# Attention's row maxima as b + relu(a - b) on half the columns, with the relu on ScalarE, and the output bias as a row added by a matmul

## The chip, the core and the metric

The kernel runs on one core of one Trainium2 chip. The metric is the device time of one execution in microseconds (us), the median of several runs. The core's engines are named as in the profile: PE (matrix multiplication), DVE (VectorE, element-wise operations and reductions), ACT (ScalarE, functions of one input), POOL (GpSimd) and SP (here the queue that issues most DMAs). PEld is the loading of weights into PE.

## What is computed

The reference is one decoder layer on x of 8 x 512 x 512 in f32, with three parts, each followed by a layer norm of the sum:

```python
x = layernorm(x + mamba(x))                       # a state-space scan, 1024 channels, 16 states
x = layernorm(x + attention(x, ctx_1024, mask))   # 16 heads of 32
x = layernorm(x + experts(x))                     # 32 experts, 4 per token, and a shared one
```

The change touches the attention:

```python
scores = einsum('bnlh,bnph->bnlp', qm, km) / sqrt(32)
scores = where(mask, scores, -1e8)
attn = softmax(scores, axis=-1)
out = einsum('bnlp,bnph->bnlh', attn, vm)
out = out.reshape(B, L, 512) @ Wo.T + bo
```

The softmax needs the largest score of every row, over 512 keys, for each of 8 batches, 16 heads and 512 queries.

## The kernel before

`program` runs three stages: `layers` (the scan and the attention, up to about 3750 us), `experts`, and `finish`. Only `layers` is changed.

**The order of the work.** The main loop of `layers` goes over 16 chunks (8 batches, two halves of 256 positions each), and in each over 32 steps of the scan. A step has on DVE a multiplication `steps_in` (L494), the scan itself (L501) and a multiplication `collect` (L510), each over 1024 or 1028 columns; on ACT four exponentials, `decays` (L480), into one of two buffers `l_da`; and on PE matmuls (L521) that add up the states in `py`. Between these the loop puts side work: the attention of the batch before, as a list of `units`, each with a weight. A step takes as many units as its share of the weights allows. A unit runs its matmuls at once and gives back a function, its second half, which is issued when the next unit comes (`settle`); a second half may give back a third. The last batch has no scan beside it, and its units run one after the other. On top of this the framework orders the instructions of each engine by its own planner, so that neighbours in the source need not be neighbours in a queue. Every queue is worked off in order.

**The attention of a batch.** `sources` makes values and keys from the context; `keys` (L732) adds the bias and applies the mask on DVE (L741) and writes the keys to DRAM (`kd`, 512 x 512). `spread` (L799) brings the queries and keys of two heads into `qa` and `ka`, three buffers of each in turn. Head j takes 64 partitions: 32 with the head, one with the mask's fill (`filld`), and more for the maximum that is to be subtracted. For each of 8 pairs of heads and 4 blocks of 128 queries, `maximum` (L811) makes the scores of 128 queries and 512 keys for two heads with two matmuls (L819) into a PSUM tile of 128 x 1024, and its second half reduces them to two maxima on DVE (L821). `negate` brings the four blocks' maxima into a row of `qa`. Then `weigh` (L839) makes the same scores transposed (L845), ACT takes their exponentials into `eT` (L849), and `gather` (L853) multiplies with the values (L861). The maxima run six units ahead of the exponentials. The PSUM pool for scores, `l_pss`, has two buffers, which `maximum` and `weigh` share; `eT` has two buffers in pool `l_p2`; many tiles of 128 x 512 share two buffers under the name `row` in `l_p3`.

`output` (L908) multiplies with Wo (`dense`, L753, four matmuls at L756), adds x (L919) and then the bias (L920), which `l_bo` holds in all 128 partitions. `biases` (L1037 on) adds the values' bias, multiplied with Wo, to it (L1055). `prepare` (L432) multiplies with `w_dt`, 32 partitions of 1024 columns (L437).

Of the kernel before, what the change touches and what calls it, by code (L numbers as in the profile page):

```python
# [17 lines left out]
P = 128  # L18
# [14 lines left out]
NB = 4  # L33
NPB = 3

NH = 16
# [53 lines left out]
def layers(ctx, tc, a, x1d, filld, based, xbuf, arm):  # L90
# [88 lines left out]
    w_x = const("w_x", [P, CC, RANK + 2 * NST], rows(a["x_proj_w"]))  # L179
    w_dt = const("w_dt", [RANK, DI], a["dt_proj_w"])  # L180
    b_dt = const("b_dt", [P, CC], a["dt_proj_b"])
# [4 lines left out]
    bv = cp.tile([P, DC], F32, name="l_bv")  # L186
    bo = cp.tile([P, D], F32, name="l_bo")
    wg = cp.tile([P, DC, E], F32, name="l_wg")
# [47 lines left out]
    for i in range(NPB):  # L236
        qas.append(cp.tile([P, S], F32, name=f"l_qa{i}"))
        kas.append(cp.tile([P, S], F32, name=f"l_ka{i}"))
        for t in (qas[i], kas[i]):
            for r0 in (HD, 2 * HD + HD):  # L240
                nc.gpsimd.memset(t[r0 : r0 + HD], 1.0 if t is qas[i] else 0.0)
# [21 lines left out]
    def later_constants():  # L263

        nc.sync.dma_start(
            aneg.rearrange("p c j g -> p (c j) g"),
            a["A_log"].rearrange("(b c) (s g) -> (c s) b g", c=QP, s=NQ),
        )
        for i in range(NPB):
            for r0 in (HD + 1, 2 * HD + HD + 1):  # L270
                nc.sync.dma_start(
                    kas[i][r0 : r0 + 1, :].rearrange("p (c t) -> p c t", c=DC),
                    ones[0:1, :].unsqueeze(1).to_broadcast([1, DC, P]),
                )
        nc.sync.dma_start(bq, a["bq"])
        nc.sync.dma_start(bk, a["bk"])
        nc.sync.dma_start(bv, a["bv"].rearrange("(c p) -> p c", p=P))
        nc.sync.dma_start(bo, a["bo"].partition_broadcast(P))
        nc.sync.dma_start(wg, rows(a["wg"]))
# [152 lines left out]
    def prepare(q, f):  # L432

        ps = psm.tile([P, 2, T], F32, tag="mm", name="ps_dt")
        for i in range(2):
            c = 2 * q + i
            nc.tensor.matmul(  # L437
                ps[:, i, :], w_dt[:, c * P : (c + 1) * P], f["xd"][0:RANK, :], start=True, stop=True
            )
# [267 lines left out]
    def sources(b):  # L707
# [3 lines left out]
        def begin():  # L711
            load("Wv")
            st["cT"] = cT = quad("s2", "cT")
            nc.sync.dma_start(cT, rows(a["ctx"][b]))
            st["mk"] = mk = p1.tile([P, S], U8, tag="mk", name="mk")
            nc.sync.dma_start(mk, a["mask"][b : b + 1, :].to_broadcast([P, S]))
            kept[b] = [dp.tile([S, D], F32, tag="vd", name="vd"), dp.tile([D, S], F32, tag="kd", name="kd")]

# [13 lines left out]
        def keys(oc):  # L732
            if oc == 0 and b:
                load("Wq")
            w, cT = loaded["Wk"], st["cT"]
            ps = dense(lambda dc: w[:, dc, oc * P : (oc + 1) * P], lambda dc: cT[:, dc, :])

            def put():

                k = p3.tile([P, D], F32, tag="row", name="k")  # L740
                nc.vector.scalar_tensor_tensor(k, ps, bk[:, oc : oc + 1], st["mk"], ALU.add, ALU.mult)  # L741
                nc.sync.dma_start(kept[b][1][oc * P : (oc + 1) * P, :], k)

            return put
# [7 lines left out]

    def dense(lhs, rhs):  # L753
        ps = psm.tile([P, S], F32, tag="mm", name="ps_p")
        for dc in range(DC):
            nc.tensor.matmul(ps, lhs(dc), rhs(dc), start=(dc == 0), stop=(dc == DC - 1))  # L756
        return ps

    def units(b):
# [39 lines left out]
        def spread(i):  # L799
# [3 lines left out]
            for j in range(2):  # L803
# [4 lines left out]
                nc.sync.dma_start(ka[r1 + HD : r1 + HD + 1, :], filld[b : b + 1, :])  # L808
                nc.sync.dma_start(qa[r1 + HD + 1 : r1 + HD + 2, :], ka[r1 + HD + 2 : r1 + HD + 3, :])

        def maximum(i, lt):  # L811
# [5 lines left out]
            for j in range(2):  # L817
                r = slice(j * 2 * HD, (j + 1) * 2 * HD)
                nc.tensor.matmul(ps[:, j, :], qa[r, lt * P : (lt + 1) * P], ka[r, :], start=True, stop=True)  # L819
            mx = st["mx", i]  # L820
            return lambda: nc.vector.tensor_reduce(mx[:, lt, :].unsqueeze(2), ps, AX.X, ALU.max) and None  # L821

# [85 lines left out]
        def output(lt):  # L908
# [6 lines left out]
            w, attT = loaded["Wo"], st["attT"]  # L915
            pp = dense(lambda dc: attT[:, dc, lt * P : (lt + 1) * P], lambda dc: w[:, dc, :])

            def add_up():
                nc.vector.tensor_tensor(xr, pp, xr, ALU.add)  # L919
                nc.vector.tensor_tensor(st["x2"][lt], xr, bo, ALU.add)  # L920
                if lt == SC - 1:
                    return layernorm(nc, sm, st["x2"], st["x2"], "ln3")
# [114 lines left out]
    def biases():  # L1037
# [6 lines left out]
        nc.vector.tensor_scalar(fl[0:B, :], fl[0:B, :], -1.0, 1e8, ALU.add, ALU.mult)  # L1044
        nc.sync.dma_start(filld, fl[0:B, :])

# [3 lines left out]
        for dc in range(DC):  # L1050
# [3 lines left out]
            )  # L1054
        nc.vector.tensor_tensor(bo, bo, psb, ALU.add)  # L1055

# [538 lines left out]
def program(tc, a, out):  # L1595
    nc = tc.nc
    with tc.tile_pool(name="dram", bufs=1, space=DRAM) as dram, tc.tile_pool(name="one", bufs=1) as one:
        x1d = dram.tile([N, D], F32, name="x1d")
        filld = dram.tile([B, S], F32, name="filld")

# [42 lines left out]
```

## Time and profile before

| | us |
|---|---|
| runs (median, lowest, highest) | 5266.59, 5265.96, 5273.14 |
| profiled execution, its own time | 5280.81 |
| its span | 5279.1 |
| DVE busy in the span | 4173.3 |
| PE busy in the span | 4501.0 |
| ACT busy in the span | 2586.6 |
| L821, the maxima, 256 instructions | 309.8 |
| L849, the exponentials, 256 instructions | 258.7 |

The profile is of one execution. A group of instructions is given by its line in the kernel, its engine, its operation, the tile that it writes and those that it reads, the shapes and the count; then follow its busy time, the mean duration of one in ns, the engine's idle time before them, and what ended that idle time ("<-PE py L521" says that line 521 on PE did). A waits view adds up, for each pair of a waiting line and the line waited for, the time in total, the number of times and the longest. A timeline has the start, the length, the engine, the line and the operation, with the idle time before it in brackets. An f32 matmul appears as two records.

### The profile page before, as it was taken

Reading aid. Unit: us, or ns where it says so; the run is one execution under the profiler, and the core shown is the slowest. Engines: PE = TensorE matmul, PEld = TensorE weight load, DVE = VectorE, ACT = ScalarE, POOL = GpSimd, SP = SyncE. Lnnn points to the kernel's source line nnn. Section 1 sums busy time; section 2 is a strip of 40 time slices with the busy share of each in tenths; the row PEclk is TensorE's granted clock in tenths of the full one; section 3 lists DMA queues with packets and bytes.
Section 4 is the critical chain, followed back from the end, with each engine's and each line's share of the span. In section 5 each row is a group of like instructions: output and inputs, shape, how many; then the busy total and the mean of one; then the engine's idle time right before and its main releaser. Section 6 shows DMA issues by size and latency. Waiting matters only on the chain. (4 is left out here: it accounts for less than half of the span.)

```text
span 5279.1 us, 54371 instructions
## 1 busy us (share of the span) xinstructions
PE 4501.0 (85%) x17184; PEld 2464.4 (47%) x17184; DVE 4173.3 (79%) x5351; ACT 2586.6 (49%) x5771; POOL 588.5 (11%) x426
## 2 busy tenths in 40 slices
PE   6768889888888888888897888888899999999995
PEld 3324234333433433343342343332478888877774
DVE  7999898989989898998999899874355666656555
ACT  5565565665656556565655556533122333323233
POOL 1000002002000200200020020010112121111111
PEclk8879899999999999999999999999899999999997
DMA  8885345435533634544463554432244444444444
GB/s 236 266 229 157 72 119 177 115 101 148 160 95 91 208 88 109 171 128 102 105 201 78 125 173 113 106 115 93 93 129 125 128 139 132 128 116 132 117 123 151
DMA packets 486438, 711.64 MB, mean 135 GB/s; under 512 B 121576, under 2 KB 205064, under 8 KB 483952
## 3 DMA queue, kind: packets, MB, share of 16 engines
q1 hardware_dynamic: 449984, 626.90, 41.0%
q0 software_dynamic: 33280, 67.81, 5.8%
q10 hardware_dynamic: 2736, 11.54, 0.5%
q8 instruction: 221, 3.62, 0.3%
q14 instruction: 217, 1.78, 0.1%
HBM read 391.24 MB, written 164.79 MB: 105 GB/s over the span
## 5 line engine op out<-in xcount | busy, mean ns | idle before, releaser
L480 ACT ACTIVATE l_da<-rep,l_aneg 128x256 f32<-128x256 f32 x2048 | 893.5, 499 | 950.0 <-DVE h L501 885.6
L501 DVE TENSOR_TENSOR_SCAN h<-l_da,h 128x1028 f32<-128x1028 f32 x512 | 1163.3, 2285 | 21.6 <-ACT l_da L480 19.1
L494 DVE TENSOR_TENSOR h<-rep,bc 128x1024 f32<-128x1024 f32 x512 | 612.3, 1212 | 109.1 <-PE py L521 91.2
L510 DVE TENSOR_TENSOR h<-h,bc 128x1024 f32<-128x1024 f32 x512 | 616.8, 1211 | 2.1
L521 PE MATMUL py<-h,l_fold 128*32 128x512 f32 x2048 | 371.9, 649 | 108.1 <-DVE h L510 89.7
L819 PE MATMUL ps_s<-l_ka,l_qa 64*128 64x512 f32 x1024 | 331.8, 719 | 134.5 <-DVE mx L821 134.2
L1334 PE MATMUL ps_h<-xT,w 128*128 128x224 f32 (+3 forms) x1536 | 380.0, 397 | 38.4 <-issue 31.4
L1427 POOL DMA_INDIRECT based<-y,xe x160 | 272.5, 1703 | 1168.5 <-ACT y L1406 439.1
L821 DVE TENSOR_REDUCE mx<-ps_s 128x2 f32<-128x1024 f32 x256 | 309.8, 1214 | 67.8 <-PE ps_s L819 67.4
L861 PE MATMUL po<-eT,l_va 128*64 128x512 f32 x1024 | 302.5, 672 | 49.0 <-ACT eT L849 44.2
L1334 PEld LDWEIGHTS ps_h<-xT,w 128*128 128x128 f32 x1536 | 295.4, 193 | 103.8 <-issue 46.7
L845 PE MATMUL ps_t<-l_qa,l_ka 64*128 64x512 f32 x1024 | 305.5, 668 | 23.5 <-ACT eT L849 23.2
L849 ACT ACTIVATE eT<-ps_t 128x1024 f32<-128x1024 f32 x256 | 258.7, 1014 | 127.9 <-PE ps_t L845 127.8
L694 POOL DMA_INDIRECT xbuf<-x2t,dest x128 | 217.1, 1696 | 864.6 <-DVE dest L679 763.9
L343 PE MATMUL ps_z<-xnT,wm 128*128 128x256 f32 x1024 | 237.9, 389 | 28.4 <-DVE o L561 24.2
L756 PE MATMUL ps_p<-x2T,wa 128*128 128x512 f32 x512 | 241.9, 627 | 21.8 <-ACT hT L950 15.5
L552 PE MATMUL po<-wm,zs 128*128 128x512 f32 x512 | 248.5, 640 | 13.1 <-DVE z L963 11.8
L1334 PE MATMUL ps_h<-t,s 128*128 128x224 f32 (+3 forms) x1024 | 248.1, 393 | 5.8 <-DVE hT L1355 5.8
L1355 DVE TENSOR_TENSOR hT<-ps_h,p 128x224 f32<-128x224 f32 (+3 forms) x128 | 55.2, 432 | 248.9 <-PE ps_h L1334 248.8
L343 PE MATMUL ps_x<-xnT,wm 128*128 128x256 f32 x1024 | 245.7, 392 | 5.0 <-ACT xnT L332 3.2
L343 PEld LDWEIGHTS ps_z<-xnT,wm 128*128 128x128 f32 x1024 | 195.2, 193 | 90.2 <-DVE o L561 37.4
L343 PEld LDWEIGHTS ps_x<-xnT,wm 128*128 128x128 f32 x1024 | 195.8, 195 | 80.2 <-issue 43.7
(239 smaller groups left out, 6989.4 us busy)
## 6 DMA issues: line engine op xcount, KB each, us to landing
w<-in_w SPq DMA_DIRECT2D x93, 1024.0 KB
wm<-in_in_proj_w SPq DMA_DIRECT2D x128, 512.0 KB
rep<-dt SPq DMA_DIRECT2D x256, 256.0 KB
rep<-dtx SPq DMA_DIRECT2D x256, 256.0 KB
xbuf<-zero SPq DMA_DIRECT2D x32, 1362.5 KB
xe<-xbuf SPq DMA_DIRECT2D x32, 1362.5 KB
wm<-in_out_proj_w SPq DMA_DIRECT2D x64, 512.0 KB
wa<-in_sw SPq DMA_DIRECT2D x24, 1024.0 KB
```

The costliest lines, as they stand in the source:

```text
L343: nc.tensor.matmul(ps[:, i, :], w[:, dc, i * P : (i + 1) * P], f["xnT"][:, dc, :], start=(dc == 0), stop=(dc == DC - 1),)
L480: nc.scalar.activation(da[:, n, 1:], dt[:, j, i, :], AF.Exp, scale=aneg[:, 2 * q + i, 2 * jj + j, g : g + 1])
L494: nc.vector.tensor_tensor(h[:, :, 1:], dtx.rearrange("p j i t -> p (j i) t"), f["bc", g][0], ALU.mult)
L501: nc.vector.tensor_tensor_scan(flat, da.rearrange("p n t -> p (n t)"), flat, 0.0, ALU.mult, ALU.add)
L510: nc.vector.tensor_tensor(h[:, :, 0:T], h[:, :, 1:], f["bc", g][1], ALU.mult)
L521: nc.tensor.matmul(f["py"][j * QP : (j + 1) * QP, :, :], fold, hs[j // 2][:, 2 * (j % 2) : 2 * (j % 2) + 2, 0:T], start=False, stop=g == N ...
L819: nc.tensor.matmul(ps[:, j, :], qa[r, lt * P : (lt + 1) * P], ka[r, :], start=True, stop=True)
L821: return lambda: nc.vector.tensor_reduce(mx[:, lt, :].unsqueeze(2), ps, AX.X, ALU.max) and None
L845: nc.tensor.matmul(ps[:, j, :], ka[r, kc * P : (kc + 1) * P], qa[r, :], start=True, stop=True)
L861: nc.tensor.matmul(po[j * 2 * HD : (j + 1) * 2 * HD, :], va[:, kc, i, j * HD : (j + 2) * HD], eT[:, j, :], start=(kc == 0), stop=(kc == SC ...
L1334: nc.tensor.matmul(ps, w[:, n, r * P : (r + 1) * P], x[:, n, 0:cols], start=not more and n == 0, stop=n == 1, skip_group_check=more,)
L1427: put = nc.gpsimd.indirect_dma_start(out=based, out_offset=bass.IndirectOffsetOnAxis(ap=xe.bitcast(I32)[:, j, D + E :], axis=0), in_=ys[j] ...
```

## The change

The largest of two numbers is written as max(a, b) = b + relu(a - b). For each head, a is the scores of keys 0 to 255 and b those of keys 256 to 511. The keys in DRAM and in `ka`, and the mask's fill, get a third part of 256 columns that holds the first half less the second. The two matmuls of `maximum` then use columns 256 to 767 of `ka`, so that PSUM holds b and a - b. The second half of the unit takes relu(a - b) of both heads on ACT into `up`, a tile under the name `eT`; a new third part adds b and takes the maximum along the row on DVE, with one instruction per head.

The bias is no longer held in 128 partitions. It lies in one row, beside 31 rows of zeros, in a part of the tile of `w_dt`, which is made 64 partitions high; `dense` adds it with a fifth matmul of 32 rows of ones, and the second addition of `output` goes.

```diff
-    w_dt = const("w_dt", [RANK, DI], a["dt_proj_w"])
+    w_dt = cp.tile([2 * RANK, DI], F32, name="l_w_dt")
+    nc.sync.dma_start(w_dt[0:RANK, :], a["dt_proj_w"])
+    bo = w_dt[RANK : 2 * RANK, 0:D]
+    nc.gpsimd.memset(bo, 0.0)
...
-    bo = cp.tile([P, D], F32, name="l_bo")
...
-        kas.append(cp.tile([P, S], F32, name=f"l_ka{i}"))
+        kas.append(cp.tile([P, S + HS], F32, name=f"l_ka{i}"))
...
-                nc.sync.dma_start(kept[b][1][oc * P : (oc + 1) * P, :], k)
+                nc.sync.dma_start(kept[b][1][oc * P : (oc + 1) * P, 0:S], k)
+                less = p3.tile([P, D], F32, tag="row", name="less")[:, 0:HS]
+                nc.vector.tensor_tensor(less, k[:, 0:HS], k[:, HS:], ALU.subtract)
+                nc.sync.dma_start(kept[b][1][oc * P : (oc + 1) * P, S:], less)
...
-    def dense(lhs, rhs):
+    def dense(lhs, rhs, row=None):
         ps = psm.tile([P, S], F32, tag="mm", name="ps_p")
         for dc in range(DC):
-            nc.tensor.matmul(ps, lhs(dc), rhs(dc), start=(dc == 0), stop=(dc == DC - 1))
+            nc.tensor.matmul(ps, lhs(dc), rhs(dc), start=(dc == 0), stop=(dc == DC - 1 and row is None))
+        if row is not None:
+            nc.tensor.matmul(ps, ones[RANK : 2 * RANK, :], row, start=False, stop=True)
...
-                nc.tensor.matmul(ps[:, j, :], qa[r, lt * P : (lt + 1) * P], ka[r, :], start=True, stop=True)
+                nc.tensor.matmul(ps[:, j, :], qa[r, lt * P : (lt + 1) * P], ka[r, HS:], start=True, stop=True)
             mx = st["mx", i]
-            return lambda: nc.vector.tensor_reduce(mx[:, lt, :].unsqueeze(2), ps, AX.X, ALU.max) and None
+
+            def ramp():
+                up = p2.tile([P, 2, S], F32, tag="eT", name="up")[:, :, 0:HS]
+                nc.scalar.activation(up, ps[:, :, HS:], AF.Relu)
+
+                def largest():
+                    for j in range(2):
+                        nc.vector.tensor_tensor_reduce(
+                            up[:, j, :], ps[:, j, 0:HS], up[:, j, :], 1.0, -3e38, ALU.add, ALU.max, mx[:, lt, j : j + 1]
+                        )
+
+                return 0, largest
+
+            return ramp
...
-            pp = dense(lambda dc: attT[:, dc, lt * P : (lt + 1) * P], lambda dc: w[:, dc, :])
+            pp = dense(lambda dc: attT[:, dc, lt * P : (lt + 1) * P], lambda dc: w[:, dc, :], bo)
 
             def add_up():
-                nc.vector.tensor_tensor(xr, pp, xr, ALU.add)
-                nc.vector.tensor_tensor(st["x2"][lt], xr, bo, ALU.add)
+                nc.vector.tensor_tensor(st["x2"][lt], pp, xr, ALU.add)
...
-        nc.sync.dma_start(filld, fl[0:B, :])
+        nc.sync.dma_start(filld[:, 0:S], fl[0:B, :])
+        less = p3.tile([P, D], F32, tag="row", name="less")[0:B, 0:HS]
+        nc.vector.tensor_tensor(less, fl[0:B, 0:HS], fl[0:B, HS:], ALU.subtract)
+        nc.sync.dma_start(filld[:, S:], less)
...
-        nc.vector.tensor_tensor(bo, bo, psb, ALU.add)
+        row = p3.tile([P, D], F32, tag="row", name="bo")[0:1, :]
+        nc.sync.dma_start(row, a["bo"].unsqueeze(0))
+        nc.vector.tensor_tensor(row, row, psb[0:1, :], ALU.add)
+        nc.sync.dma_start(bo[0:1, :], row)
```

More of the change, by code (lines that the diff above doesn't have):

```diff
@@ L34 @@
 NPB = 3
+HS = S // 2
 NH = 16
@@ L271, in later_constants @@
                 nc.sync.dma_start(
-                    kas[i][r0 : r0 + 1, :].rearrange("p (c t) -> p c t", c=DC),
+                    kas[i][r0 : r0 + 1, 0:S].rearrange("p (c t) -> p c t", c=DC),
                     ones[0:1, :].unsqueeze(1).to_broadcast([1, DC, P]),
@@ L277, in later_constants @@
         nc.sync.dma_start(bv, a["bv"].rearrange("(c p) -> p c", p=P))
-        nc.sync.dma_start(bo, a["bo"].partition_broadcast(P))
         nc.sync.dma_start(wg, rows(a["wg"]))
@@ L437, in prepare @@
             nc.tensor.matmul(
-                ps[:, i, :], w_dt[:, c * P : (c + 1) * P], f["xd"][0:RANK, :], start=True, stop=True
+                ps[:, i, :], w_dt[0:RANK, c * P : (c + 1) * P], f["xd"][0:RANK, :], start=True, stop=True
             )
@@ L716, in begin @@
             nc.sync.dma_start(mk, a["mask"][b : b + 1, :].to_broadcast([P, S]))
-            kept[b] = [dp.tile([S, D], F32, tag="vd", name="vd"), dp.tile([D, S], F32, tag="kd", name="kd")]
+            kept[b] = [dp.tile([S, D], F32, tag="vd", name="vd"), dp.tile([D, S + HS], F32, tag="kd", name="kd")]
         def values(pc):
@@ L808, in spread @@
                 nc.sync.dma_start(ka[r1 + HD : r1 + HD + 1, :], filld[b : b + 1, :])
-                nc.sync.dma_start(qa[r1 + HD + 1 : r1 + HD + 2, :], ka[r1 + HD + 2 : r1 + HD + 3, :])
+                nc.sync.dma_start(qa[r1 + HD + 1 : r1 + HD + 2, :], ka[r1 + HD + 2 : r1 + HD + 3, 0:S])
         def maximum(i, lt):
@@ L1598, in program @@
         x1d = dram.tile([N, D], F32, name="x1d")
-        filld = dram.tile([B, S], F32, name="filld")
+        filld = dram.tile([B, S + HS], F32, name="filld")
         based = dram.tile([N, D], F32, name="based")
```

## The prediction

> **What bounds the kernel now.** The page's busy shares come first, then the busy times by stretch, because the shares are averages over stages with different limits.
>
> ```profile
> PE 4501.0 (85%) x17184; PEld 2464.4 (47%) x17184; DVE 4173.3 (79%) x5351; ACT 2586.6 (49%) x5771; POOL 588.5 (11%) x426
> ```
> ```profile
> 2500.00:3000.00 500.00, 423.05 (x1548) 179.71 (x1546) 452.32 (x498) 300.57 (x665) 42.29 (x33) 0.93 0.47 127
> ...
> 3600.00:3700.00 100.00, 98.72 (x413) 29.77 (x409) 45.03 (x41) 44.36 (x54) 0.00 (x0) 1.00 0.17 43
> ```
>
> The columns are the stretch, its length, busy time of PE, PEld, DVE, ACT and POOL, the granted clock, and DMA. Up to about 3590 us the scans and the attention of the batch before run side by side. There DVE is busy 452 of 500 us (90%), PE 85%, ACT 60%. In the attention part of one batch (2335 to 2410 us) DVE is busy 71.57 of 75 us (95%), PE 62.81 and ACT 45.03. The last batch's attention runs alone from 3600 to 3700 us, and there PE is busy 98.72 of 100 us: DVE's price hardly counts in that stage. The experts after it are not touched.
>
> Next, the groups by line with their shapes, and DVE's waits, both for 600 to 3400 us.
>
> ```profile
> L501 DVE TENSOR_TENSOR_SCAN h<-l_da,h 128x1028 f32<-128x1028 f32 x396 | 900.0, 2286 | 19.9 <-ACT l_da L480 17.6 <-ACT h L488 1.4
> ...
> L821 DVE TENSOR_REDUCE mx<-ps_s 128x2 f32<-128x1024 f32 x201 | 243.0, 1213 | 12.8 <-PE ps_s L819 12.4
> ...
> L920 DVE TENSOR_TENSOR x2t<-xr,l_bo 128x512 f32<-128x512 f32 x24 | 16.3, 677 | 0.0
> ```
> ```profile
> DVE h L494 <- PE py L521: 89.7, 38, 7.0
> ...
> DVE h L501 <- ACT l_da L480: 17.6, 6, 3.4
> ```
>
> The maxima take 243 us of the bounding engine in this stretch. DVE waits seldom for the maxima's scores (12.8 us) and seldom for ACT's decays (17.6 us).
>
> What an instruction costs a busy DVE is the distance from start to start, not its duration, so I read the timeline of DVE:
>
> ```profile
> 2166.95 0.42 DVE L612 TENSOR_TENSOR g_eq<-g_gs 128x256 f32<-128x256 f32 x1
> 2167.29 0.42 DVE L614 TENSOR_TENSOR g_eq<-g_gs 128x256 f32<-128x256 f32 x1
> 2167.62 0.42 DVE L613 TENSOR_TENSOR g_eq<-g_eq,l_lower 128x256 f32<-128x256 f32 x1
> ...
> 2175.12 0.08 DVE L634 MATCH_VALUE_LOAD l_masked<-l_tops,l_masked 128x8 f32 x1
> 2175.18 0.18 DVE L634 MATCH_REPLACE8 l_masked<-l_tops,l_masked 128x36 f32<-128x36 f32 x1
> ```
> ```profile
> 2358.15 1.21 DVE L821 TENSOR_REDUCE mx<-ps_s 128x2 f32<-128x1024 f32 x1
> 2359.28 1.21 DVE L510 TENSOR_TENSOR h<-h,bc 128x1024 f32<-128x1024 f32 x1
> ```
>
> A two-input operation on 256 columns costs 0.335 us (2167.62 less 2167.29, and its neighbour), one on 512 costs 0.60 us (L460 to the next start, 2180.70 to 2181.31), and a maximum of 1024 columns 1.13 us (2358.15 to 2359.28).
>
> **The change, part by part.**
>
> *1. The maxima.* All 256 instructions of L821 go. Each is replaced by two add-and-maximum instructions on 256 columns, and in the changed kernel's recorded order each of these is followed by a second instruction that writes the accumulator out: four for one. No row shows either. The main one streams two inputs as L612 does, and L821 shows that a running maximum goes at full rate (1.13 us for 1024 columns, 1.1 ns each), so I take L612's 0.335 us; the ends are that and 0.48 us, the mean duration of L377 (476 ns) with no overlap. The write-out lies between nothing and 0.19 us, a small operation that waits for the one before (L74 to L75); MATCH_VALUE_LOAD, 0.06 us, is a short helper of the same kind. I take 0.13 us. One maximum then costs 2 x (0.335 + 0.13) = 0.93 us, with ends 0.67 and 1.34. Of the 256, 224 lie beside scans (seven batches of 32): 224 x (1.13 - 0.93) = 45 us off DVE; by the ends, 103 us off or 47 us on.
>
> [...]
>
> *2. The relu on ACT.* 256 instructions of 512 columns out of PSUM, like L389 (569 ns): 146 us more on ACT, about 18 us in each batch's attention, which raises ACT there from 60% to some 71%. It is hidden by DVE as long as no scan waits for it. In the changed order `up` takes buffers from the two of `eT`, and 175 of 256 exponentials (L849) now have a wait for DVE, the maximum that reads the same buffer; before none has. Queued behind such an exponential on ACT are the decays (L480) for a later scan. I counted, in the changed order, DVE's work between that maximum and the scan against ACT's work up to its decays: nearly everywhere DVE has over 4 us more to do, and at one place per batch it has 2.3 us against ACT's 4.1 us. Six such places and a smaller one: 13 us on. The ends are 0 (ACT further ahead) and 26 us (L501's longest wait for ACT, 3.4 us, at each, rounded up).
>
> *3. The keys.* 32 differences of 256 columns on DVE at 0.335 us: 11 us on. The row buffers must now let two DMAs go per key; the wait for such a DMA (L741 for a row's write) was 1.0 us at longest, two times. Bounds 0 to 32 us, taken 2, since a key comes about once in a scan's step. SP issues 32 more writes at 0.38 us (L742) and longer fetches of the keys, beside other work.
>
> *4. The bias as a row.* L920 goes: 32 times 0.60 us, 28 beside scans, 17 us off DVE. It adds 32 matmuls of 512 columns; a full one of L756 takes 0.86 us (two records of 0.43 us), so 28 x 0.86 = 24 us on PE, hidden by DVE at 95%. In the last batch PE is the limit: 4 x 0.86 = 3 us on, and about 1 us off for the last L920. The row is made once in the first batch, by one addition on one partition and two DMAs; as with other set-up there, I take it at 0, and at 3 us if the matmuls that share its tile wait for the second DMA.
>
> *5. The last batch.* The timeline of it:
>
> ```profile
> 3613.70 1.13 PE L819 MATMUL ps_s<-l_ka,l_qa 64*128 64x512 f32 x4
> ...
> 3614.90 1.23 DVE L821 TENSOR_REDUCE mx<-ps_s 128x2 f32<-128x1024 f32 x1 [2.79 <-PE ps_s L819]
> ...
> 3615.79 1.02 ACT L849 ACTIVATE eT<-ps_t 128x1024 f32<-128x1024 f32 x1 [1.40 <-PE ps_t L845]
> ...
> 3617.59 1.02 PE L845 MATMUL ps_t<-l_qa,l_ka 64*128 64x512 f32 x4
> ```
>
> The scores end at 3614.83. With the relu (0.57 us) and the pair (0.93 us) after it, the exponential starts at about 3616.5 in place of 3615.79 and ends at 3617.5, so its PSUM comes free as the next L845 is due: 0 to 0.4 us late, 28 times, 0 to 11 us; taken 5 us. A pair at 1.34 us would make it some 16 us.
>
> **The sum.** Beside the scans DVE loses 45 - 11 + 17 = 51 us. I count 0.8 of it, since DVE's other 5 to 10% of idle time stays and PE is next at 85%: 41 us off. Against it 13 + 2 + 5 + 2 = 22 us on. Net 19 us off the profiled execution's 5280.81 us (span 5279.1), and the same off the median of 5266.59 us, which lies 14 us below it: 5247 us.
>
> **The rivals.**
>
> *Freed time turns into waits.* For: the chain of one maximum gains an engine, and PE already waits for maxima (121.5 us at L819, 600 to 3400 us), with the scans' products queued behind; DVE's largest wait, 89.7 us, is for these products. Against: that wait is there mostly outside the attention part; between 2030 and 2140 us it is 0.5 us. If half of the 51 us converts, 26 off and 22 on: 5263 us.
>
> *The pair is as dear as the maximum it replaces.* This is the slower side, and it is one mechanism: the fixed price of four instructions in place of one. By the sum above, the time is unchanged at a price of 1.04 us for a maximum and is over 0.2% slower from about 1.10 us, so 0.55 us for one main instruction with its write-out. At 1.2 us: 16 us on DVE, 6 off for the rest, 22 of waits and 4 more in the last batch: 5303 us. At 1.34 us, 47 - 6 + 22 + 11 = 74 on: 5340 us. For: no row shows the operation. Against: L612 and L821.
>
> *The whole gain comes through.* With a write-out of almost nothing (pair 0.70 us) and no new wait, 224 x 0.43 + 6 = 102, of which 0.8 is 82 off: 5185 us. For: the counted slack is over 4 us nearly everywhere.
>
> **How the numbers follow.** A difference under 0.2% (11 us) can't be told from none here. Chances: forecast as worked out (5230 to 5256) 0.38; the whole gain 0.12; freed time turned into waits 0.18; the dear pair 0.32. Faster 0.49 takes the first two less a little, same 0.19, slower 0.32. The range runs from 5190, near the full gain, to 5325, short of the pair's upper end; for the faster cases alone it is 5190 to 5256.
>
> **What would show it.** In the changed profile: the main instruction at about 0.42 us and start to start of a pair 0.93 us (right), over 1.1 us (wrong, slower); relu at 0.57 us; DVE's waits for `l_da` up by about 13 us; DVE's share beside the scans still 90%; the last attention longer by some 5 us. A rise of DVE's wait for py would favour the first rival. The prediction is wrong if the pair costs over 1.04 us, or if ACT's queue holds up scans in every step.

## The result, and the profile after

| | before | after |
|---|---|---|
| median of 9 runs each on one chip, us | 5271.14 (5265.96 to 5279.98) | 5286.59 (5276.85 to 5290.6) |
| ratio, with its 95% interval | | 1.0024 (1.0016 to 1.0033) |
| profiled execution, span, us | 5279.1 | 5285.1 |
| DVE, PE, ACT busy in the span, us | 4173.3, 4501.0, 2586.6 | 4062.7, 4544.7, 2703.5 |

The changed kernel takes 0.24% longer, some 13 to 15 us. I had forecast 5247 us. Lines after the change are up to 25 higher: scores L826, relu L831, pair L835, scan L503, the multiplication before it L496, py L521 and L523, the row's matmul L763.

First the busy shares of the changed kernel's page, then its busy times by stretch (stretch, length, PE, PEld, DVE, ACT, POOL, clock, DMA):

```profile
PE 4544.7 (86%) x17248; PEld 2457.0 (46%) x17248; DVE 4062.7 (77%) x6120; ACT 2703.5 (51%) x6011; POOL 573.1 (11%) x427
```
```profile
2500.00:3000.00 500.00, 428.58 (x1535) 182.15 (x1534) 438.46 (x605) 317.09 (x697) 38.56 (x30) 0.93 0.47 130
3600.00:3700.00 100.00, 90.69 (x342) 29.92 (x344) 30.14 (x122) 48.74 (x69) 0.64 (x3) 0.94 0.36 116
```

DVE lost 111 us of work in the whole span, and the kernel is longer all the same. Beside the scans DVE's busy share fell from 90% to 88% while PE's rose from 85% to 86%: the freed time was not used.

What the new pair costs, in the groups for 600 to 3400 us and in the timeline of DVE:

```profile
L496 DVE TENSOR_TENSOR h<-rep,bc 128x1024 f32<-128x1024 f32 x392 | 471.1, 1217 | 129.8 <-PE py L523 122.3 <-DMA rep<-dtx 5.5 <-PE ps_t L865 1.4
L835 DVE CUSTOM_DVE_ANT_0 up<-ps_s,up 128x256 f32<-128x256 f32 x408 | 155.3, 418 | 111.3 <-ACT up L831 110.8
...
L835 DVE DVE_READ_ACCUMULATOR2_ANT mx<- 128x1 f32 x408 | 34.0, 83 | 0.0
```
```profile
2063.89 0.42 DVE L835 CUSTOM_DVE_ANT_0 up<-ps_s,up 128x256 f32<-128x256 f32 x1 [0.15 <-ACT up L831]
2064.24 0.08 DVE L835 DVE_READ_ACCUMULATOR2_ANT mx<- 128x1 f32 x1
2064.24 0.42 DVE L835 CUSTOM_DVE_ANT_0 up<-ps_s,up 128x256 f32<-128x256 f32 x1
2064.58 0.08 DVE L835 DVE_READ_ACCUMULATOR2_ANT mx<- 128x1 f32 x1
2064.58 0.16 DVE L75 TENSOR_TENSOR m<-v,r 128x2 f32<-128x2 f32 x1
```

From start to start the pair takes 0.69 us (2063.89 to 2064.58): the write-out begins with the next instruction (both at 2064.24 us) and adds nothing to that. That is the cheap end of my bounds. But beside the 155 us of the main instructions stand 111 us in which DVE waited for the relu. The waits of DVE and then of PE, for the same stretch:

```profile
DVE h L496 <- PE py L523: 122.3, 58, 6.5
DVE up L835 <- ACT up L831: 110.8, 47, 5.7
```
```profile
PE ps_s L826 <- DVE mx L835: 146.9, 74, 3.3
PE py L521 <- DVE zs L537: 33.3, 18, 5.0
```

DVE's wait for py was 89.7 us before. PE's wait for the maxima before:

```profile
PE ps_s L819 <- DVE mx L821: 121.5, 87, 2.8
```

Both engines wait longer, each for the other. In this stretch DVE's busy time fell from 2541.73 to 2444.81 us, 97 us, in the same 2800 us: its idle time grew by as much. One of the waits, from the timeline of all engines (DVE's instruction before it ended at 2066.66):

```profile
2063.79 2.08 PE L521 MATMUL py<-xs,l_ident 128*128 128x512 f32 x2 [4.99 <-DVE zs L537]
...
2069.53 0.27 PE L848 MATMUL ps_m<-l_ident,mx 128*2 128x128 f32 x1
...
2069.73 1.13 PE L826 MATMUL ps_s<-l_ka,l_qa 64*128 64x512 f32 x4
...
2070.33 1.50 ACT L82 ACTIVATE xt<-xt,less,r 128x512 f32<-128x512 f32 x2
...
2071.74 0.57 ACT L831 ACTIVATE up<-ps_s 128x512 f32<-128x512 f32 x1
...
2072.34 0.42 DVE L835 CUSTOM_DVE_ANT_0 up<-ps_s,up 128x256 f32<-128x256 f32 x1 [5.68 <-ACT up L831]
```

The pair stands first in DVE's queue and waits 5.68 us. The scores come late because PE is busy with what is ahead of them, from 2063.79 to 2069.73 us, and that was late itself: PE had just waited 4.99 us for DVE (first line). Then ACT finishes a layer norm (L82, 1.50 us for its two instructions), and only then takes the relu. The scan behind the pair waits too, until 2073.23 us.

**By stage.** The trace splits the time at three events: the first instruction, the start of the last scan, and the first and last scatter of the experts (times here count from the trace's zero, 11 us ahead of the span's). I profiled both kernels a second time (the runs `g1_before_again` and `g2_after_again` below). The two profiles of one kernel differ by 5 to 7 us at the last scan, so a smaller difference there between single profiles says nothing:

| | last scan starts at | last scan to first scatter | first to last scatter |
|---|---|---|---|
| before, two profiles | 3529.7, 3524.3 | 321.4, 320.8 | 1383.2, 1379.5 |
| after, two profiles | 3552.9, 3546.1 | 332.6, 332.9 | 1354.0, 1354.4 |
| difference | +22 to +23 | +11 to +12 | -25 to -29 |

The change loses some 34 us in the stages that it touches, and 25 to 29 us come back in the experts, which it does not touch. That return repeats; I come to it at the end. In the runs below the experts take from 1353 to 1392 us, though no edit touches them. The totals of kernels with different programs therefore hide up to 40 us of something else, and beside the medians I give the stages.

### The profile page after: what moved, and what is told of

Same layout as the page of the kernel before. It is cut to its first block, busy times and chain, and to the rows that moved or that the text cites. A ratio compares the mean times of both kernels' runs of the same rounds, so it can differ in the third digit from the quotient of the medians.

```text
span 5285.1 us, 55910 instructions
## 1 busy us (share of the span) xinstructions
PE 4544.7 (86%) x17248; PEld 2457.0 (46%) x17248; DVE 4062.7 (77%) x6120; ACT 2703.5 (51%) x6011; POOL 573.1 (11%) x427
## 4 chain that ended last, share of the span: by engine, by line
PE 40%; DVE 38%; issue 8%; ACT 7%; DMA 4%; SPq 1%; POOL 0%; DVEq 0%; ACTq 0%; POOLq 0%
DVE h L503 15%; PE ps_h L1359 15%; PE ps_o L1359 7%; DVE h L496 6%; DVE h L512 6%; PE ps_p L761 4%; DVE xs L379 2%; PE po L554 2%; PE py L523 2%; DVE up L835 2%; ACT l_da L482 2%; PE ps_s L826 1%; PE ps_t L1325 1%; PE po L881 1%; PE ps_t L865 1%
## 5 line engine op out<-in xcount | busy, mean ns | idle before, releaser
L503 DVE TENSOR_TENSOR_SCAN h<-l_da,h 128x1028 f32<-128x1028 f32 x512 | 1167.8, 2291 | 6.2 <-ACT l_da L482 2.3
L496 DVE TENSOR_TENSOR h<-rep,bc 128x1024 f32<-128x1024 f32 x512 | 614.6, 1216 | 147.0 <-PE py L523 131.0
L523 PE MATMUL py<-h,l_fold 128*32 128x512 f32 x2048 | 390.1, 672 | 109.9 <-DVE h L512 93.3
L826 PE MATMUL ps_s<-l_ka,l_qa 64*128 64x512 f32 x1024 | 320.2, 690 | 162.3 <-DVE mx L835 154.2
L835 DVE CUSTOM_DVE_ANT_0 up<-ps_s,up 128x256 f32<-128x256 f32 x512 | 195.3, 419 | 187.6 <-ACT up L831 186.7
L826 PEld LDWEIGHTS ps_s<-l_ka,l_qa 64*128 64x128 f32 x1024 | 88.4, 194 | 326.1 <-issue 137.4
L761 PE MATMUL ps_p<-x2T,wa 128*128 128x512 f32 x512 | 230.8, 603 | 4.0 <-ACT hT L969 3.3
```

Of the source, the lines that this page charges most:

```text
L496: nc.vector.tensor_tensor(h[:, :, 1:], dtx.rearrange("p j i t -> p (j i) t"), f["bc", g][0], ALU.mult)
L503: nc.vector.tensor_tensor_scan(flat, da.rearrange("p n t -> p (n t)"), flat, 0.0, ALU.mult, ALU.add)
L523: nc.tensor.matmul(f["py"][j * QP : (j + 1) * QP, :, :], fold, hs[j // 2][:, 2 * (j % 2) : 2 * (j % 2) + 2, 0:T], start=False, stop=g == N ...
```

## The experiments

Each was timed in five rounds beside the kernel before, whose medians were 5272.2 (e), 5273.6 (f), 5276.5 (g) and 5268.7 us (h) in the four groups. "Edit" is against the kernel before or the changed one, as said.

**Which part loses?** I began with four theories: freed DVE time is worth what I forecast but the relu eats it (A), freed DVE time is worth little (B), the buffers that relu and exponentials share cost it (C), or the bias row does.

*e1, against before:* the maximum over half the columns (not the true maximum of the row; the scores are still made in full).

```diff
-            return lambda: nc.vector.tensor_reduce(mx[:, lt, :].unsqueeze(2), ps, AX.X, ALU.max) and None
+            return lambda: nc.vector.tensor_reduce(mx[:, lt, :].unsqueeze(2), ps[:, :, 0:256], AX.X, ALU.max) and None
```

> The kernel before, whose maximum reads 256 of each head's 512 columns: it leaves out the first... the second half of the scores from the maximum, and no other engine is touched. DVE's price of a maximum should fall from 1.13 to about 0.60 us, 119 us less beside the scans. Theory A (DVE bounds; in the changed kernel the freed time is lost because each maximum now goes through ACT, whose relu comes late): 80 to 110 us faster than before. Theory B (DVE's busy time does not bound; another chain, over PE, does): within 15 us of before, with DVE's idle time up by about 100 us.

Measured 5254.66 us, ratio 0.9963 (0.9949 to 0.9977); last scan at 3503.4. The maxima fall from 1.21 to 0.68 us; 224 of them free 119 us of DVE beside scans, and the kernel gains 17 to 20 us, about 0.15 of it (by the last scan 21 to 26 us, about 0.2). Where the rest went, in DVE's waits for 600 to 3400 us:

```profile
DVE h L494 <- PE py L521: 162.2, 56, 6.5
```

Before, that wait was 89.7 us. DVE finished earlier and waited longer for PE. No relu is in this kernel, so my conversion of 0.8 fails here by itself.

*e2, against after:* no relu; the pair adds a constant tile to the scores in PSUM and writes there (not the true maximum).

```diff
-                nc.scalar.activation(up, ps[:, :, HS:], AF.Relu)
...
-                            up[:, j, :], ps[:, j, 0:HS], up[:, j, :], 1.0, -3e38, ALU.add, ALU.max, mx[:, lt, j : j + 1]
+                        ps[:, j, 0:HS], ps[:, j, 0:HS], w_x[:, 0:4, :].rearrange("p c n -> p (c n)"),
+                        1.0, -3e38, ALU.add, ALU.max, mx[:, lt, j : j + 1],
```

> The changed kernel without the relu: the pair on DVE adds a constant tile to the scores of the second half of the keys, so the first half is left out of the maximum. The pair's price on DVE should stay at 0.69 us, ACT's 120 us and the wait for it are gone. Theory A: 60 to 90 us faster than before, DVE's waits for ACT at the pair gone. Theory B: within 15 us of before. If the price of the pair or the other parts of the change were to blame, it would stay at about 15 us slower.

Measured 5315.04 us, ratio 1.0079 (1.0064 to 1.0093); last scan at 3574.9. Taking the relu away does not mend it: the scans become 22 to 29 us longer than with it. DVE's wait for py is 148.5 us in place of 122.3. But the edit does more than leave the relu out: a pair that writes back to PSUM is dearer where its two main instructions stand next to each other (0.52 us from one to the next against 0.34; the last section has the rows' times), and DVE's busy time in the whole span is 4081 us against 4063. So e2 does not say what the relu costs by itself; it shows that the loss is not mended by leaving it out.

*e3, against before:* the bias row alone (row, fifth matmul, no second addition; maxima as before).

```diff
-            pp = dense(lambda dc: attT[:, dc, lt * P : (lt + 1) * P], lambda dc: w[:, dc, :])
+            pp = dense(lambda dc: attT[:, dc, lt * P : (lt + 1) * P], lambda dc: w[:, dc, :], bo)
...
-                nc.vector.tensor_tensor(xr, pp, xr, ALU.add)
-                nc.vector.tensor_tensor(st["x2"][lt], xr, bo, ALU.add)
+                nc.vector.tensor_tensor(st["x2"][lt], pp, xr, ALU.add)
```

> The kernel before with the bias as a row alone: one addition of 512 columns less on DVE per output block (0.60 us, 32 times), one matmul more on PE. Theory A and B: 0 to 15 us faster. Theory D (this part is the loss: PE, or the bias tile shared with the matrix of the time step, holds things up): 10 us slower or more.

Measured 5284.05 us, ratio 1.0025 (1.0016 to 1.0035): in the total as much as the whole change. By stage it is half of it: last scan at 3534.8 (+5 to +10), then 332.7 (+11 to +12), experts 1367.6 (-12 to -16).

*e4, against after:* the relu's results in four buffers of their own.

```diff
-                up = p2.tile([P, 2, S], F32, tag="eT", name="up")[:, :, 0:HS]
+                if i == 0 and lt == 0:
+                    st["ups"] = quad("s1", "ups")
+                up = st["ups"][:, (i * SC + lt) % 4, :].rearrange("p (j t) -> p j t", j=2)
```

> The changed kernel with the relu's output in four buffers of its own, in a large tile that lies idle between the queries and the output, so that no exponential waits for a maximum and no relu for a matmul with the values. Theory C (the loss comes from the two buffers that relu and exponential share: ACT waited 47 us for DVE at the exponential between 600 and 3400 us): 30 us or more faster than the changed kernel, so faster than before. Theory A (the relu is late because of the queue in front of it, on PE and ACT): within 10 us of the changed kernel, and DVE still waits over 80 us for the relu between 600 and 3400 us.

Measured 5291.52 us, ratio 1.0042 (1.0029 to 1.0055); last scan at 3554.7. The shared buffers are not the cause: theory C falls. DVE still waits 107.2 us for the relu between 600 and 3400 us.

**Is it PE?** After these four my theory, P, was that beside the scans PE's queue is the bound as much as DVE, and that the fifth matmul is what loses.

*f1, against after:* the row's matmul left out (the bias is missing from the sum; it is zero in these inputs).

```diff
-            pp = dense(lambda dc: attT[:, dc, lt * P : (lt + 1) * P], lambda dc: w[:, dc, :], bo)
+            pp = dense(lambda dc: attT[:, dc, lt * P : (lt + 1) * P], lambda dc: w[:, dc, :])
```

> The changed kernel without the fifth matmul of each output block: the bias is left out of the sum altogether, neither PE nor DVE adds it. Theory P (beside the scans PE's order is as much the bound as DVE; the row matmul loses, the maxima gain a little): the loss goes, 5262 to 5271 us, some 15 to 24 us faster than the changed kernel and a little faster than the kernel before. Theory M (the new maxima, with their relu and their longer keys, lose by themselves): 5280 us or more.

Measured 5282.22 us, ratio 1.0015 (1.0004 to 1.0026); last scan at 3549.2, then 324.6, experts 1355.4. That is theory M's number, and theory P falls. The matmul costs 8 us in the last batch, and beside the scans nothing: 3549.2 lies between the changed kernel's two profiles.

*f2, against before:* a fifth matmul with a row of zeros (`none`, beside the delta weights), both additions kept.

```diff
+    none = w_dt[RANK : 2 * RANK, 0:D]
+    nc.gpsimd.memset(none, 0.0)
...
+            pp = dense(lambda dc: attT[:, dc, lt * P : (lt + 1) * P], lambda dc: w[:, dc, :], none)
```

> The kernel before with a fifth matmul of a row of zeros in each output block, and both additions on DVE kept: PE's work alone is added, 32 times 0.6 to 0.9 us beside some 5271 us. Theory P (the matmul itself is the cost, DVE's second addition was worth nothing): as the bias row alone, 5282 to 5290 us. Theory Q (the cost of the bias row lies in its making, or in the tile shared with the delta weights): within 4 us of the kernel before.

Measured 5324.47 us, ratio 1.0095 (1.008 to 1.0109), far more than either theory: last scan at 3551.6 (+22 to +27), then 331.5 (+10), experts 1392.1. Why the same matmul costs 22 us beside the scans here and none in e3 or f1 I can't say: the second addition behind it is one difference, the order of the queues another, and no run parts them.

*f4, against before:* the second addition left out (bias missing), no matmul added.

```diff
-                nc.vector.tensor_tensor(xr, pp, xr, ALU.add)
-                nc.vector.tensor_tensor(st["x2"][lt], xr, bo, ALU.add)
+                nc.vector.tensor_tensor(st["x2"][lt], pp, xr, ALU.add)
```

> The kernel before without the second addition (L920): the bias is left out of the sum, DVE has 28 times 0.60 us = 17 us less beside the scans, PE is as before. Theory P, with the conversion of 0.16 that the half maximum showed: 2 to 5 us faster, 5266 to 5270 us. My prediction's conversion of 0.8: 13 us faster, 5258 us.

Measured 5277.41 us, ratio 1.0012 (1.0003 to 1.0021); last scan at 3534.8. 17 us less on DVE gained nothing: the last scan is 5 to 10 us later, which is little more than the two profiles of one kernel differ. The order of the instructions on PE, DVE and ACT changed too; whether that took the gain is not shown. The last scan is where e3 has it, so in e3 the matmul was hidden beside the scans.

*f3, against e1:* scores of 256 columns only, so the half maximum needs half of PE's work for them. The shift that the softmax takes off is the largest of the first 256 keys; a softmax does not depend on the shift, but a row whose first 256 keys are all masked would overflow, so this is no general replacement.

```diff
-                nc.tensor.matmul(ps[:, j, :], qa[r, lt * P : (lt + 1) * P], ka[r, :], start=True, stop=True)
+                nc.tensor.matmul(ps[:, j, 0:256], qa[r, lt * P : (lt + 1) * P], ka[r, 0:256], start=True, stop=True)
```

> The kernel before with maxima over 256 of 512 columns, and with the scores computed for these 256 columns alone: to the half maximum (which freed about 119 us of DVE and gained 17 us) it takes about half of 320 us of PE beside the scans away. Theory P: PE is the co-bound, so 60 to 120 us faster than the half maximum alone, 5135 to 5195 us. Theory D (DVE alone bounds, and the gain was lost to the length of the chain of one maximum): 5235 to 5255 us.

Measured 5073.77 us, ratio 0.9613 (0.9601 to 0.9625), the fastest of the study; last scan at 3333.7. It is 181 us faster than e1, more than theory P asked. Between 600 and 3200 us DVE waited 139.1 us for py in e1; here little of that is left:

```profile
DVE h L494 <- PE py L521: 18.4, 20, 1.8
```

*g3, against f3:* the half maximum taken twice.

```diff
+                for _ in range(2):
+                    nc.vector.tensor_reduce(mx[:, lt, :].unsqueeze(2), ps[:, :, 0:256], AX.X, ALU.max)
```

> The kernel before with the scores computed for 256 of 512 columns, and the half maximum taken twice, so that DVE has about the work of before and PE alone is relieved. With the kernel before (5272 us), the half maximum (5255 us) and the half maximum with half the scores (5074 us) it makes a table of two by two. Theory P (the period beside the scans follows PE's queue): 5075 to 5115 us. Theory C (PE and DVE are a bound together, either one alone gains little): 5180 to 5250 us.

Measured 5174.54 us, ratio 0.9811 (0.9795 to 0.9827), just under what theory C of that expectation says. The pages of g3 and then f3:

```profile
PE 4404.1 (85%) x17184; PEld 2463.8 (48%) x17184; DVE 4181.8 (81%) x5607; ACT 2593.9 (50%) x5778; POOL 589.4 (11%) x426
```
```profile
PE 4368.1 (86%) x17184; PEld 2449.8 (48%) x17184; DVE 4032.3 (79%) x5351; ACT 2589.9 (51%) x5778; POOL 594.5 (12%) x426
```

DVE's busy time is that of the kernel before in the one (4182 and 4173 us) and that of e1 in the other (4032 and 4039). The table of two by two:

| median, us | maxima in full or twice | half maxima | gained on DVE |
|---|---|---|---|
| scores of 512 columns | 5272 (before) | 5254.7 (e1) | 17 |
| scores of 256 columns | 5174.5 (g3) | 5073.8 (f3) | 101 |
| gained on PE | 98 | 181 | |

The same relief of DVE is worth 17 us with the scores at full width and 101 us with half of them. DVE's busy time falls by 16.8 us a batch in the upper row (411.4 to 394.6) and by 18.3 in the lower (411.9 to 393.6); over the seven batches beside scans that is 118 and 128 us, of which 0.15 and 0.79 come through. By stage the picture is the same: the last scan comes 21 to 26 us earlier in the upper row and 94 us in the lower, and the experts of all four kernels take 1380 to 1386 us. My 0.8 is the number for the lower row. The busy shares don't tell the rows apart: PE is at 86% of the span in e1 and in f3. Half of the scores' columns take work off PE and also bring each maximum its scores sooner; which of the two counts, the table does not say.

**What else holds the change back?** *g4, against after:* scores of 256 columns (keys 256 to 511), which relu and pair both read (not the true maximum); all else of the change stays.

```diff
-                nc.tensor.matmul(ps[:, j, :], qa[r, lt * P : (lt + 1) * P], ka[r, HS:], start=True, stop=True)
+                nc.tensor.matmul(ps[:, j, 0:HS], qa[r, lt * P : (lt + 1) * P], ka[r, HS:S], start=True, stop=True)
...
-                nc.scalar.activation(up, ps[:, :, HS:], AF.Relu)
+                nc.scalar.activation(up, ps[:, :, 0:HS], AF.Relu)
```

> The changed kernel with the scores of 256 columns alone (keys 256 to 511), from which both the relu and the pair read: PE has half the work for the scores, relu, pair, the keys' third part and the bias row stay as in the change. The maximum is not the true one. Theory L (the relu between the scores and the maximum costs by its length, since PE's next scores wait for the buffer; about 26 us): 5105 to 5135 us. Rival (with PE relieved there is slack for the chain, and only the bias row and the keys are left): 5080 to 5100 us.

Measured 5162.4 us, ratio 0.9786 (0.9771 to 0.9802): 88 us behind f3, more than either expectation, though DVE's busy time beside the scans differs by only 3 us a batch (396.7 and 393.6). Four runs take the parts of the change out of g4, or put the pair into f3:

*h1:* g4 with f1's edit. *h2:* g4 with e2's edit. *h3:* g4 without the keys' third part:

```diff
-                less = p3.tile([P, D], F32, tag="row", name="less")[:, 0:HS]
-                nc.vector.tensor_tensor(less, k[:, 0:HS], k[:, HS:], ALU.subtract)
-                nc.sync.dma_start(kept[b][1][oc * P : (oc + 1) * P, S:], less)
```

*h4:* f3 with the pair of h2 in place of the reduction.

> The changed kernel with half scores (5162 us), without the fifth matmul of each output block: the bias is left out of the sum. If the 88 us to the half maximum with half scores are the matmul's: 5075 to 5100 us. If it costs here what it cost beside full scores, 5 to 15 us: 5147 to 5157 us.

> The changed kernel with half scores, without the relu: the pair adds a constant tile to the scores in PSUM and writes them back there. Theory L (the relu costs by lengthening the way from the scores to the maximum, on which PE's next scores wait): 40 to 70 us faster than with it, 5090 to 5120 us. Rival (as beside full scores, where the kernel without relu was slower than with it): 5155 us or more.

> The changed kernel with half scores, without the third part of the keys: no differences on DVE, no writes of them, and the keys are fetched with 512 columns as before (relu and pair read the scores of keys 256 to 511 as in the kernel it is compared with). If the third part costs DVE's 11 us and a few waits: 5147 to 5157 us. If its transfers hold up the scores: 5130 us or less.

> The kernel before with half scores and the pair in place of the half reduction, adding a constant tile in PSUM: no relu, no third part, the bias by DVE as before. If the pair is worth what its 0.69 us say (the half reduction takes about as long): within 15 us of 5074 us. If the pair itself is what holds the change back: 5100 us or more.

| | median, us | ratio to before (interval) | last scan at | to first scatter |
|---|---|---|---|---|
| f3, half reduction | 5073.77 | 0.9613 (0.9601 to 0.9625) | 3333.7 | 313.8 |
| h4, f3 with the pair | 5107.63 | 0.9695 (0.9681 to 0.9708) | 3374.8 | 311.4 |
| h2, g4 without relu | 5129.92 | 0.9732 (0.9719 to 0.9745) | 3386.5 | 319.2 |
| h3, g4 without third part | 5134.71 | 0.9746 (0.9731 to 0.9761) | 3405.0 | 329.8 |
| h1, g4 without row matmul | 5145.56 | 0.9774 (0.976 to 0.9787) | 3426.5 | 317.6 |
| g4 | 5162.4 | 0.9786 (0.9771 to 0.9802) | 3426.1 | 329.9 |

h1 and h4 came out near the second of their two expectations, h2 and h3 between theirs. No single part is the cause. With PE relieved, the scans lose 41 us to the pair in place of the half reduction (h4 against f3), 40 to the relu (g4 against h2), 21 to the third part (g4 against h3), and nothing to the row's matmul (g4 against h1), which costs 12 us in the last batch. Some of the 41 is the price of a pair that works in PSUM, as DVE's busy time is 397.3 us a batch in h4 and 393.6 in f3, 26 us over seven batches. The first three overlap: they add up to 102, and g4 is 92 us behind f3. At full width the relu's share had the other sign (e2), so these shares don't carry over to the change as it stands.

**Controls.** *g1* is the kernel before and *g2* the changed one, without an edit, for a second profile each.

> The kernel before, unchanged, profiled a second time. In the two profiles the changed kernel lost 23 us up to the last scan and 11 us in the last batch, and won 29 us in the experts, which the change does not touch; there the granted clock was at half for 41 us in 9 pieces before, and for 8 us in 2 pieces after. Theory G (these falls of the clock come and go from one execution to the next): the last scan starts again at 3530 us, give or take 6, and the experts take some other time between 1354 and 1392 us. Rival (the experts' time belongs to the kernel): 1383 us again, within 4.

> The changed kernel, profiled a second time. Theory G: the last scan starts again at 3553 us, give or take 6, and the experts take some other time between 1354 and 1392 us. Rival: 1354 us again, within 4.

One execution each: 5272.4 and 5281.36 us. The scans come out as expected, 3524.3 and 3546.1; for the experts the rival was right: 1379.5 and 1354.4 us, each kernel's own figure again.

## Why the prediction was wrong, step by step

1. **The pair** (0.93 us taken, 0.67 to 1.34 allowed): 0.69 us. A mis-sized term, in the change's favour: 224 x 0.44 = 99 us off DVE in place of 45. In the rows above it is 0.34 to 0.35 us from the start of one main instruction to the start of what follows it, while the instruction lasts 0.42, and the write-out falls into the overlap; I had put 0.13 us on top for it.
2. **The conversion** ("I count 0.8 of it, since DVE's other 5 to 10% of idle time stays and PE is next at 85%") is the step that failed. e1 shows 0.15 with no other part of the change in it, and the table of two by two shows why: the relief of DVE is worth 101 us once PE makes half of the scores, and 17 us before. A share of 90% on DVE and 85% on PE looked like an order, first and second. By the waits above they are a ring: the multiplication before a scan (L494) waits for py on PE to free its buffer (89.7 us in the stretch before), PE's scores wait for the maxima on DVE (121.5 us), and each queue is worked off in order (of the instructions that can be matched by their lines, 4095 on DVE, 2713 on ACT and 10408 on PE, the profile before has none out of the order of the program). My first rival, "freed time turns into waits", had the mechanism, and the rise of DVE's wait for py that was to favour it came (89.7 to 122.3 us); but I let half of the time convert. I had held against that rival that the wait lies mostly outside the attention part, by 0.5 us between 2030 and 2140 us. That reading was wrong: this window has only 5 of the batch's 32 maxima. From the first of them to the last, 1877 to 2071 us in the kernel before, stands

```profile
DVE h L494 <- PE py L521: 11.6, 4, 6.8
```

   and 0.4 us in the 134 us ahead of them (1743 to 1877 us). In e1 it is 23.5 us from the first maximum of the same batch to the last (1865 to 2056 us).
3. **The relu**: 0.57 us forecast, 0.57 to 0.60 measured. I looked for its harm in the decays behind coupled exponentials (13 us). That wait, the scan's for `l_da`, shrank from 19.1 to 2.3 us in the whole span. What came is another wait: DVE itself waits for the relu, 47 times and 110.8 us in the stretch, since the pair stands in DVE's queue ahead of the scans. With half scores the kernel without the relu is 32 us faster (h2 against g4); what the wait costs at full width no run shows. I had costed the step on ACT and counted the instructions behind it there, but never asked how long the pair would wait.
4. **The bias row**: "24 us on PE, hidden by DVE at 95%" was right in outcome beside the scans (f1 and h1 are level there with the kernels that have the matmul; f2, which is not, stays unexplained). In the last batch I had 3 us on and 1 off. This is its output stage after:

```profile
3738.24 1.79 PE L761 MATMUL ps_p<-wa,attT 128*128 128x512 f32 x2 [3.64 <-DVE attT L920]
3739.96 2.07 PE L763 MATMUL ps_p<-l_w_dt,l_ones 32*128 32x512 f32 x2
3741.96 2.08 PE L761 MATMUL ps_p<-wa,attT 128*128 128x512 f32 x2
3743.97 2.07 PE L763 MATMUL ps_p<-l_w_dt,l_ones 32*128 32x512 f32 x2
```

   PE has just waited 3.64 us for the last quarter of the attention's result, and its clock is down: the row's matmul takes 2.07 us in two of the four blocks, where the granted clock is 0.53 (3738 to 3749 us), and 1.12 in the others, where it is 1.00 (3750.9 to 3757 us). I had taken 0.86, two records of L756 at 0.43 us each from start to start, which is what they take in the kernel before at a clock of 1.00; at 0.50 it is 0.85 us each. The granted clock for 3738 to 3757 us is 0.73; before, the same stage ran at 0.84. From PE's start after that wait to the last output matmul it is 18.6 us (3738.24 to 3756.8) against 10.6 before. Also mis-sized: making the row lengthens the first batch by 5 us (338.3 against 333.3 us from first scan to first scan of the next, and 338.7 in e3), where I had 0 to 3.
5. **The last batch's attention**: 5 us taken, 4.6 measured (191.1 to 195.7 us from the last scan to the last division). Right.
6. **The keys**: 11 us on DVE were there; that their third part also costs the scans by waits is shown only with half scores (21 us with the 11 in them).

So 19 us off in the sum became 34 on in the stages concerned: 22 beside the scans, 5 of them in the first batch, and 12 in the last batch. My slower rival had the right sign by the wrong mechanism: the pair was not dear. DVE's busy time fell from 411.4 to 397.7 us a batch, 96 us over seven; at e1's 0.15 that is worth some 14 us, an estimate, so that relu, pair, third part and the new order of the queues must have cost some 30 us beside the scans. How they divide at full width stays open: e2 lengthens what h2 shortens, and single profiles are good to 5 to 7 us.

## What to carry to other kernels

Two engines at 90% and 85% that feed each other in order can be one bound: before counting what a relief of the busier one is worth, look who waits for whom between them, and expect the freed time to turn up in that wait; here 0.15 of it came through, and five times as much once half of the scores on the other engine were gone. An operation that is split over a second engine must be costed by its way from the first input to the freed buffer, with the queues that it passes, and not by its busy time on each engine. And when a change moves the time by less than 1%, split the trace by stages and profile both kernels twice, since a stage that nobody touched can move by as much, as the experts did here by 25 to 29 us.

## What the hardware showed

**Stalls of PE at fixed instructions.** The experts differ by 25 to 29 us between the two kernels, in both profiles of each, with the same instructions. PE is idle in them for 71 and 73 us before and 56 and 55 after, and busy for 1312 and 1307 against 1298 and 1300. In them PE stands still now and then for 3 to 6 us, for nothing that the waits show, and at the same place in both profiled executions of a kernel. PE's timeline, the kernel before in its two profiles:

```profile
3968.86 0.81 PE L1334 MATMUL ps_o<-w,hT 128*128 128x256 f32 x3
3974.32 2.50 PE L1334 MATMUL ps_o<-w,hT 128*128 128x256 f32 x5 [4.64 <-issue]
```
```profile
3963.14 0.81 PE L1334 MATMUL ps_o<-w,hT 128*128 128x256 f32 x3
3968.32 2.50 PE L1334 MATMUL ps_o<-w,hT 128*128 128x256 f32 x5 [4.37 <-issue]
```

Both times after the third of these eight records, 134 us after the first scatter; the five that follow take 0.50 us each in place of 0.27, in the first profile at a granted clock of 0.50 (3974 to 3977 us). The changed kernel has none there; it has one after the second of eight records at 532 us after the first scatter, again in both its profiles:

```profile
4400.06 0.60 PE L1359 MATMUL ps_o<-w,hT 128*128 128x256 f32 x2
4406.15 2.93 PE L1359 MATMUL ps_o<-w,hT 128*128 128x256 f32 x6 [5.50 <-issue]
```
```profile
4394.19 0.60 PE L1359 MATMUL ps_o<-w,hT 128*128 128x256 f32 x2
4399.99 2.93 PE L1359 MATMUL ps_o<-w,hT 128*128 128x256 f32 x6 [5.20 <-issue]
```

Five of the six stalls of 3 us or more in the first profiles of the two kernels have a stretch at half clock at their end. In the experts the clock was at half for 41 and 27 us in the kernel before, and for 8 and 10 us in the changed one, in pieces of 3.4 us or small multiples of it (3.41 and 6.83 us in the first profiles). What PE waits for, the record of the single transfers suggests. The page of the kernel before sums up a queue of instructions:

```profile
q8 instruction: 221, 3.62, 0.3%
```

These are packets of 16384 bytes. In each of the 15 stalls of 3 us or more that are put down to "issue" in these four profiles and in f4's, such a packet starts during the stall, and PE goes on 2.2 to 2.6 us after its start. In the first profiles 129 and 127 of them fall into the experts, one in 11 us. I take it from this that PE stands there until its next instructions have come; no run shows that, nor why they come late at these places and not at others. That the stalls go with the program and not with the arithmetic, f4 suggests: it only leaves 32 instructions of DVE out, long before the experts, and has them at 1368 us.

**The pair's accumulator is written out beside the next instruction.** The second instruction of the pair (it lasts 83 ns after a main one that writes to SBUF, and 139 to 142 ns in h4 and e2, where the main one writes to PSUM) costs no time of its own in the changed kernel: in 248 of its 256 pairs the first write-out begins together with the second main instruction, 0.32 to 0.35 us after the first one. In e2, where the pair writes to PSUM, a second main instruction that comes next mostly starts only after the write-out: 0.52 us behind the first (2039.50 to 2040.02 us). Between 600 and 3400 us its 404 main instructions, of 425 ns each, are busy for 170.3 us and so hardly overlap, while the changed kernel's 408, of 418 ns, are busy for 155.3.
